# A graph-attention kernel on one core: later requests for block 2's rows, GpSimd's first sums beside the norms, a copy on ScalarE, and the last block's residual sums apart

## Chip, cores and metric

One core of one Trainium2 chip. The metric is device time in microseconds (us), one execution of the whole program. All arithmetic is fp32, and the matmuls decide the time: TensorE is busy for 2730.8 of the 2754.9 us of the kernel before.

## The reference, cut

x holds 128 graphs of 64 nodes with 768 features. It is normalised, passed through two attention layers over a 64 by 64 adjacency, and added to itself.

```python
h = jnp.maximum(_layernorm(x), 0.0)
for l in range(2):
    m_left  = jnp.einsum('bsh,oh->bso', h, W_left[l])
    m_right = jnp.einsum('bsh,oh->bso', h, W_right[l])
    u_left  = jnp.einsum('bih,bjh->bij', h, m_left) / temper
    u_right = jnp.einsum('bih,bjh->bij', h, m_right) / temper
    u = u_left * adj_tri + u_left * diag_mask + u_right * swapaxes(adj_tri, 1, 2)
    e = jnp.exp(u) * adj
    attention = e / (sum(e, axis=2, keepdims=True) + 1e-10)
    h_lin = jnp.einsum('bsh,oh->bso', h, W_lin[l]) + b_lin[l]
    h = relu(layer_norm(attention @ h_lin, ln_a[l], ln_b[l]))
return x + h
```

## The kernel before

The tokens are cut into 16 blocks of 512. For each layer a first pass projects a block with W_left and W_right and takes its scores; a second pass does W_lin, the context, the norm and, in layer 1, the residual sum. A projection is 15 block products instead of 18, on sums of weight blocks (`w_l`, `w_r`, `w_n`) and of token blocks (`ts`, from the transposed tokens `ht`); the products land in four PSUM banks X, Y, Z, V.

To place side work between matmuls, the program has numbered slots: two for each of the 15 products, slots 0 to 29 in the first half of a block and 30 to 59 in the second. `put(slot, f)` writes `f` there, so a larger number means a later place in the program. The residual sum of slot 22 runs behind VectorE's reads of bank X (2722.38 us behind 2721.72, kernel before).

The start (block 0): normalise, transpose on TensorE, copy out of PSUM, first sums.

```python
def scale(q0, q1):
    def deviation():
        nc.scalar.activation(sd[:, q0:q1], mv[:, q0:q1, 1], AF.Sqrt, bias=eps_in)
    def inverse():
        nc.vector.reciprocal(rs[:, q0:q1], sd[:, q0:q1])
        nc.vector.scalar_tensor_tensor(nb[:, q0:q1], mv[:, q0:q1, 0], -1.0, rs[:, q0:q1],
                                       op0=ALU.mult, op1=ALU.mult)
    return deviation, inverse
# ...
def turn(n, q):                       # transposes of one 128-row tile, then two copies
    # ...
        (nc.vector.tensor_copy if n < 2 else nc.scalar.copy)(
            to, p[:, :3 * P].rearrange("p (c a s) -> p c a s", c=3, a=2))
# ...
ws, vs = sums_w(0, "l", nc.gpsimd), sums_w(0, "l", nc.vector)
hold(KEEP["nb"][:, START[-2]:START[-2] + 1])     # GpSimd copies one column: it waits for the third nb
for f in ws[:2]:
    f()                                          # GpSimd's first two weight sums
```

The rows of the next block, in the first pass:

```python
def paced(to, f):
    nc.vector.memset(to, 0.0)         # the request f() must wait for this write
    f()

def prepare(u):
    todo = transpose_rows(l, u, sp)
    todo.append(lambda: load_h(1, l, u))
    if u + 1 < NB:
        todo.append(lambda: load_rows(l, u + 1, sp))    # 8 requests of 192 KB
    # ...
```

The last block of layer 1, and the end of the block before it, which runs beside it:

```python
def last_block(u):
    # ...
    put(20, lambda: load(0))
    for xs, slot in zip(XS[u, 1], (26, 45)):
        put(slot, lambda xs=xs: nc.gpsimd.tensor_add(xs, xs, rows["b"]))

def finish(u, r):
    # ...
    def scaled(k):
        nc.vector.scalar_tensor_tensor(zs[k], cx[k], rs[:, k:k + 1], rows["a"], op0=ALU.mult, op1=ALU.mult)
        nc.gpsimd.tensor_add(zs[k], zs[k], rows["b"])
    def done(k):
        xs = XS[u, r]
        nc.vector.scalar_tensor_tensor(xs[k], zs[k], 0.0, xs[k], op0=ALU.max, op1=ALU.add)  # residual sum
        # ... store xs[k]
        if k and u + r < NB - 1:
            residual(u + r, 1 - r)                # requests the rows of the next half: tile xr
    steps = [lambda f=f, k=k: f(k) for f in (scaled, done) for k in range(2)]
    return [inverse] + steps

# slots of inverse, scaled(0), scaled(1), done(0), done(1)
ends = ({0: ((u - 1, 0), (12, 13, 15, 22, 24)), 9: ((u - 1, 1), (28, 29, 30, 39, 41))},
        {2: ((u, 0), (44, 48, 51, 61, 62))})
```

Of the kernel before, what the change touches and what calls it, by code (L numbers as in the profile page):

```python
# [17 lines left out]
def kernel(  # L18
# [58 lines left out]
    def put(slot, *fs):  # L77
        plan.setdefault(slot, []).extend(fs)
# [164 lines left out]

    START = (0, 2, 1, 3)

    def load_rows(l, u, pool):

        XR[l, u] = []
        if (l, u) == (0, 0):

            rows = x.rearrange("(n k h) s f -> n k (h s) f", k=Q, h=PAIR)
            for g in range(2):
                t = pool.tile([P, 2, H], F32, name="x", bufs=2)
                XR[l, u].extend([t[:, 0, :], t[:, 1, :]])
            for q in START:
                nc.sync.dma_start(XR[l, u][q], rows[0, q])
            return
        for g in range(2):
            t = pool.tile([P, 2, H], F32, name="x", bufs=2)
            for a in range(4):  # L260
                i = 4 * g + a
                src = x[u * NBB + i] if l == 0 else ROWS[u][i]
                nc.sync.dma_start(t[a * 32:(a + 1) * 32], src.rearrange("(k j) h -> j k h", k=2))
            XR[l, u].extend([t[:, 0, :], t[:, 1, :]])

    def load_h(which, l, u):
        ht = HT[which, l, u] = big.tile([P, C, T], F32, name="ht")
# [11 lines left out]
    def transpose_rows(l, u, pool):  # L279

        key, xr, todo = (1, l, u), XR[l, u], []
        if l == 0:
            mv = stat.tile([P, Q, 2], F32, name="mv0", bufs=2)
            sd = stat.tile([P, Q], F32, name="sd0", bufs=2)
            rs = stat.tile([P, Q], F32, name="rs0", bufs=2)
            nb = stat.tile([P, Q], F32, name="nb0", bufs=2)
# [4 lines that stand above are left out]

                def inverse():
                    nc.vector.reciprocal(rs[:, q0:q1], sd[:, q0:q1])
                    nc.vector.scalar_tensor_tensor(nb[:, q0:q1], mv[:, q0:q1, 0], -1.0, rs[:, q0:q1],
                                                   op0=ALU.mult, op1=ALU.mult)

                return deviation, inverse

            def norm(q):
                nc.scalar.activation(xr[q], xr[q], AF.Relu, bias=nb[:, q:q + 1], scale=rs[:, q:q + 1])  # L300

            stats = [lambda q=q: mean_var(mv[:, q, :], [xr[q][:, :HH], xr[q][:, HH:]]) for q in range(Q)]
            norms = [lambda q=q: norm(q) for q in range(Q)]
            if u == 1:


                xb = pool.tile([P, H // 32, Q, 32], F32, name="xb", bufs=1)
                total, ss = (stat.tile([P, Q], F32, name=n, bufs=1) for n in ("total", "ss0"))

                def sums(q, to, **how):  # L310
                    nc.scalar.activation(xb[:, :, q, :], xr[q].rearrange("p (b j) -> p b j", j=32),  # L311
                                         accum_out=to[:, q:q + 1], **how)

                def inverse():
                    nc.scalar.activation(sd, ss, AF.Sqrt, bias=eps_in, scale=1.0 / H)
                    nc.vector.reciprocal(rs, sd)
                    nc.vector.tensor_mul(nb, total, rs)

                todo.extend([lambda q=q: sums(q, total, func=AF.Copy) for q in range(Q)])
                todo.append(lambda: nc.scalar.mul(total, total, -1.0 / H))  # L320
                todo.extend([lambda q=q: sums(q, ss, func=AF.Square, bias=total[:, q:q + 1]) for q in range(Q)])
                todo.extend([inverse, None] + norms)
            elif u:
                for f in stats + [lambda: [f() for f in scale(0, Q)]] + norms:
                    todo.extend([f, None])
            else:
                KEEP["nb"] = nb

                dev, inv = zip(*(scale(q, q + 1) for q in range(Q)))
                todo.extend([stats[START[0]], dev[START[0]]])  # L330
                for q, after in zip(START, START[1:] + (None,)):
                    if after is not None:
                        todo.append(stats[after])
                    todo.append(inv[q])
                    if after is not None:
                        todo.append(dev[after])
                    todo.append(norms[q])
        if (l, u) == (0, 0):
            ht = HT[key] = big.tile([P, C, T], F32, name="ht")

            def turn(n, q):

                if n < 2:
                    p = ps_aux.tile([P, 2, T], F32, name="aux")
                    banks = [p[:, 0], p[:, 1]]
                else:
                    banks = [ps_st.tile([P, 2 * TH], F32, name=m) for m in ("XY", "ZV")[n - 2]]
                for m, p in enumerate(banks):
                    for c in range(3):
                        nc.tensor.transpose(p[:, c * P:(c + 1) * P],  # L350
                                            xr[q][:, (3 * m + c) * P:(3 * m + c + 1) * P], KEEP["ident"])
                for m, p in enumerate(banks):
                    to = ht[:, 3 * m:3 * m + 3].rearrange("p c (a g s) -> p g c a s", a=4, g=2)
                    to = to[:, q // 2, :, q % 2 * 2:q % 2 * 2 + 2, :]
                    (nc.vector.tensor_copy if n < 2 else nc.scalar.copy)(
                        to, p[:, :3 * P].rearrange("p (c a s) -> p c a s", c=3, a=2))

            for n, q in enumerate(START):
                todo.append(lambda n=n, q=q: turn(n, q))
            todo.append(lambda: nc.sync.dma_start(KEPT[l][u], ht))  # L360
            return todo

        if (l, u) != (0, 1):
            xb = pool.tile([P, H // 32, Q, 32], F32, name="xb", bufs=1)

        def store():
            to = KEPT[l][u].rearrange("(b i) c t -> i c b t", b=4)
            for a in range(4):
                nc.sync.dma_start(to[:, :, :, a * P:(a + 1) * P],
                                  xb[a * 32:(a + 1) * 32].rearrange("i (c b) q j -> i c b (q j)", b=4))  # L370

        for q in range(Q):
            todo.append(lambda q=q: nc.vector.transpose(
                xb[:, :, q, :], xr[q].rearrange("p (b j) -> p b j", j=32)))
            todo.extend(none * ((l, u) != (0, 1)))
        todo.append(store)
        return todo

# [6 lines left out]
    def pass_one(l, aside):  # L385
        with tc.tile_pool(name=f"one{l}", bufs=2, reuse_waits="tile") as sp:
# [14 lines left out]

            def prepare(u):

                todo = transpose_rows(l, u, sp)
                todo.append(lambda: load_h(1, l, u))
                if u + 1 < NB:
                    todo.append(lambda: load_rows(l, u + 1, sp))
                todo.extend(softmax(u - 2) if u > 1 else [])
                todo.append(lambda: load_adj(u))
                todo.extend(none * ((9 if u > 1 else 15) if l else 0))  # L410
                return todo + affine(1, l, u)
# [86 lines left out]
            if l == 0:  # L498
# [18 lines left out]
                def hold(of):  # L517

                    t = stat.tile([P, 1], F32, name="hold", bufs=1)
                    nc.gpsimd.tensor_copy(t, of)  # L520
# [1 line left out]


                ws, vs = sums_w(0, "l", nc.gpsimd), sums_w(0, "l", nc.vector)
                hold(KEEP["nb"][:, START[-2]:START[-2] + 1])
                for f in ws[:2]:
                    f()
                t, w = deque(sums_t((1, 0, 0), nc.vector)), deque(vs[2:])
# [100 lines left out]
    def pass_two(l, aside):  # L629
        last = l == L - 1  # L630
        with tc.tile_pool(name=f"two{l}", bufs=2, reuse_waits="tile") as sp:
# [53 lines left out]
            def last_block(u):  # L685
# [12 lines left out]
                put(1, lambda: load(1))  # L698
                put(6, lambda: nc.gpsimd.tensor_scalar_mul(rows["-b"], rows["b"], -1.0))
                put(20, lambda: load(0))  # L700
                for xs, slot in zip(XS[u, 1], (26, 45)):
                    put(slot, lambda xs=xs: nc.gpsimd.tensor_add(xs, xs, rows["b"]))

            def finish_last(u, r):

# [155 lines left out]
            for u in range(NB):  # L861
# [21 lines left out]
                else:  # L883
                    if turn:
                        load_h(1, 1, 0)
                        put_all(28, affine(1, 1, 0), 3)
                        put_sums_t((1, 1, 0), 38, 2, 30)
                        ends = ({1: ((u - 1, 0), (13, 14, 16)), 11: ((u - 1, 1), (34, 35, 36))},
                                {4: ((u, 0), (50, 51, 52))})
                    else:  # L890
                        last_block(u)
                        ends = ({0: ((u - 1, 0), (12, 13, 15, 22, 24)), 9: ((u - 1, 1), (28, 29, 30, 39, 41))},
                                {2: ((u, 0), (44, 48, 51, 61, 62))})
                    linear(u, (0,), 0, ends[0], (1,))
                    linear(u, (1,), 30, ends[1], ())
# [52 lines left out]
```

## Time and profile before

| | before |
|---|---|
| median of the first 3 runs | 2756.12 us (2755.36 to 2756.13) |
| span of the profiled execution | 2754.9 us |
| TensorE busy | 2730.8 us, 99% |
| VectorE, ScalarE, GpSimd busy | 49%, 31%, 43% |

TensorE is full, so the time is its matmuls, which the change leaves alone, plus its pauses. Only what ends a pause of TensorE counts. The prediction below shows the three places with the largest pauses: the start, block 0's scores and the last block. Two more lines of the timeline also belong here. They are from the last block of the kernel before; the columns are start, duration, queue or engine, line, operation, tiles.

```profile
2726.89 2.52 SPq L732 DMA_DIRECT2D xr<-in_x_dram  x4
...
2732.72 2.16 DVE L816 SCALAR_TENSOR_TENSOR xr<-z,xr 128x768 f32<-128x768 f32 x1
```

The rows xr of the second half are requested from 2726.89 on, behind the second residual sum of the first half. In the transfer records the two requests for the first of its two tiles land by 2731.41; VectorE comes to them at 2732.72. So there were 1.3 us to spare (2732.72 - 2731.41).

### The profile page before, as it was taken

Reading aid. Unit: us, or ns where it says so; the run is one execution under the profiler, and the core shown is the slowest. Engines: PE = TensorE matmul, PEld = TensorE weight load, DVE = VectorE, ACT = ScalarE, POOL = GpSimd, SP = SyncE. Lnnn points to the kernel's source line nnn. Section 1 sums busy time; section 2 is a strip of 40 time slices with the busy share of each in tenths; the row PEclk is TensorE's granted clock in tenths of the full one; section 3 lists DMA queues with packets and bytes.
Section 4 is the critical chain, followed back from the end, with each engine's and each line's share of the span. In section 5 each row is a group of like instructions: output and inputs, shape, how many; then the busy total and the mean of one; then the engine's idle time right before and its main releaser. Section 6 shows DMA issues by size and latency. Waiting matters only on the chain.

```text
span 2754.9 us, 46440 instructions
## 1 busy us (share of the span) xinstructions
PE 2730.8 (99%) x18746; PEld 2343.7 (85%) x18746; DVE 1348.2 (49%) x2267; ACT 850.2 (31%) x1611; POOL 1195.0 (43%) x937
## 2 busy tenths in 40 slices
PE   9999999999999999999999999999999999999998
PEld 7888888888888888888788888888888888888886
DVE  6555445545454333333435444444444335676666
ACT  3222223222221154454621211121122214444443
POOL 3332352224223555555522344223222325887885
PEclk9999999999999999999999999999999999999999
DMA  6434433343332333343555433443344204555655
GB/s 203 121 75 97 121 82 81 87 120 93 76 76 77 102 104 121 119 146 123 152 129 150 99 75 76 109 119 78 76 98 120 59 26 146 167 165 164 178 161 144
DMA packets 234072, 310.82 MB, mean 113 GB/s; under 512 B 54146, under 2 KB 184450, under 8 KB 225666
## 3 DMA queue, kind: packets, MB, share of 16 engines
q1 hardware_dynamic: 233698, 307.45, 41.6%
q8 instruction: 149, 2.44, 0.4%
q14 instruction: 65, 0.53, 0.1%
q10 hardware_dynamic: 160, 0.39, 0.0%
HBM read 202.91 MB, written 104.86 MB: 112 GB/s over the span
## 4 chain that ended last, share of the span: by engine, by line
PE 96%; DVE 2%; ACT 1%; issue 1%; DMA 0%; SPq 0%; DVEq 0%; ACTq 0%
PE X L429 24%; PE V L429 16%; PE X L839 12%; PE Y L429 12%; PE Z L429 8%; PE V L839 8%; PE Y L839 6%; PE aux L456 5%; PE Z L839 4%; PE aux L654 2%; PE aux L677 1%; PE Y L677 0%; ACT xb L311 0%; DVE wm L470 0%; DMA x<-in_x_dram 0%
## 5 line engine op out<-in xcount | busy, mean ns | idle before, releaser
L155 POOL TENSOR_TENSOR ts<-ht 128x512 f32<-128x512 f32 x441 | 587.6, 1342 | 1223.0 <-DMA ht<-h 503.2
L203 ACT ACTIVATE m<-X 128x512 f32<-128x512 f32 (+1 forms) x256 | 151.7, 593 | 1089.9 <-PE X L429 571.2
L155 POOL TENSOR_TENSOR ts<-ht,ts 128x512 f32<-128x512 f32 x189 | 249.1, 1326 | 135.5 <-PE X L839 60.5
L155 DVE TENSOR_TENSOR m<-m,V 128x512 f32<-128x512 f32 (+1 forms) x256 | 173.4, 677 | 268.0 <-PE V L429 267.9
L155 DVE TENSOR_TENSOR m<-m,X 128x512 f32<-128x512 f32 (+1 forms) x256 | 162.9, 678 | 248.9 <-PE X L429 248.3
L839 PE MATMUL X<-w_n,ts 128*128 128x256 f32 x1024 | 244.2, 380 | 0.8 <-ACT hl L203 0.6
L429 PE MATMUL X<-ts,w_l 128*128 128x256 f32 x1024 | 242.7, 380 | 0.8 <-DVE ts L155 0.7
L429 PE MATMUL X<-ts,w_r 128*128 128x252 f32 (+1 forms) x1024 | 238.8, 376 | 0.1
L155 DVE TENSOR_TENSOR m<-m,Z 128x512 f32<-128x512 f32 (+1 forms) x128 | 87.5, 684 | 307.0 <-ACT m L203 248.7
L839 PEld LDWEIGHTS X<-w_n,ts 128*128 128x128 f32 x1024 | 191.5, 190 | 32.9 <-issue 3.1
L429 PEld LDWEIGHTS X<-ts,w_l 128*128 128x128 f32 x1024 | 192.0, 190 | 31.0 <-DVE m L155 2.7
L429 PEld LDWEIGHTS X<-ts,w_r 128*128 128x128 f32 x1024 | 192.0, 190 | 26.4 <-DVE m L155 0.5
L275 ACT ACTIVATE ht<-ht,b_col,a_col 128x512 f32<-128x512 f32 x192 | 143.5, 804 | 147.0 <-DMA ht<-h 147.0
L839 PE MATMUL Y<-w_n,ts 128*128 128x256 f32 x768 | 182.5, 379 | 0.0
L429 PE MATMUL Y<-ts,w_l 128*128 128x256 f32 x768 | 181.5, 379 | 0.2 <-DVE w_l L155 0.2
L429 PE MATMUL Y<-ts,w_r 128*128 128x252 f32 (+1 forms) x768 | 179.1, 376 | 0.0
L839 PEld LDWEIGHTS Y<-w_n,ts 128*128 128x128 f32 x768 | 145.8, 190 | 20.4 <-issue 0.6
L429 PEld LDWEIGHTS Y<-ts,w_l 128*128 128x128 f32 x768 | 145.8, 190 | 20.3 <-DVE w_l L155 0.6
L429 PEld LDWEIGHTS Y<-ts,w_r 128*128 128x128 f32 x768 | 145.9, 190 | 17.4
L155 DVE TENSOR_TENSOR hl<-hl,V 128x512 f32<-128x512 f32 (+1 forms) x136 | 89.1, 655 | 129.4 <-PE V L839 112.1
L805 POOL TENSOR_TENSOR z<-z,b 128x768 f32<-128x768 f32 x62 | 112.1, 1818 | 80.5 <-DVE z L802 80.5
L203 ACT ACTIVATE hl<-X 128x512 f32<-128x512 f32 (+1 forms) x135 | 78.0, 577 | 222.0 <-PE X L839 218.9
(165 smaller groups left out, 4741.1 us busy)
## 6 DMA issues: line engine op xcount, KB each, us to landing
ht<-h SPq DMA_DIRECT2D x63, 1536.0 KB, 7.1
h<-xb SPq DMA_DIRECT2D x124, 384.0 KB, 6.0
z<-z SPq DMA_DIRECT2D x128, 192.0 KB, 3.1
x<-z SPq DMA_DIRECT2D x128, 192.0 KB, 8.5
x<-in_x_dram SPq DMA_DIRECT2D x120, 192.0 KB, 8.3
xr<-in_x_dram SPq DMA_DIRECT2D x120, 192.0 KB, 3.7
out_dram<-xr SPq DMA_DIRECT2D x120, 192.0 KB, 2.7
adj<-in_adj_dram SPq DMA_DIRECT2D x64, 128.0 KB, 2.8
```

Of the source, the lines that this page charges most:

```text
L155: (eng.tensor_add if sign == "+" else eng.tensor_sub)(o, a, b)
L203: nc.scalar.activation(to(o), p, AF.Copy, scale=1.0 if sign == "+" else -1.0)
L275: nc.scalar.activation(ht, ht, AF.Relu, bias=cols[1][:, c:c + 1], scale=cols[0][:, c:c + 1])
L429: nc.tensor.matmul(p[:, g], w[ORDER[i][0]][:, c, g * P:(g + 1) * P], b()[t][:, c, :].rearrange(bs, s=S)[:, :, :ns], start=(new and g == c ...
L456: nc.tensor.matmul(p[h * S + e:h * S + e + 32, q, e:e + 95], ht[:, c, b * S + e:b * S + e + 32], mb[:, e:e + 95], start=(c == 0), stop=(c ...
L654: nc.tensor.matmul(cx[k][i, m, :HH], at[j, q, :], hl[j, q, m * HH:(m + 1) * HH], start=True, stop=True)
L677: nc.tensor.matmul(parts[r, k][n][i], at[j, q, :], hl[j, q, cut], start=True, stop=True)
L805: nc.gpsimd.tensor_add(zs[k], zs[k], rows["b"])
L839: nc.tensor.matmul(p[:, n], b[t][:, c, r * P:(r + 1) * P], w[s][:, c, :], start=(i in FIRST and i not in PRELOAD and n == c == 0), stop=(c ...
```

## The change

Its intent: to let GpSimd's first two weight sums run beside the norms; to have one of the first tile's two copies done by ScalarE; to request block 2's rows not before block 0's scores but behind them, so that they don't compete with TensorE's own instruction fetch (in the kernel before, a page of instructions started only at 73.24 us, as the data ended, and TensorE paused for 1.76 us); and to keep the residual sums of the last block but one, and GpSimd's bias adds, from running side by side (there a sum takes 2.02 us beside an add and 0.94 without; the prediction below shows what that costs).

```diff
--- before.py
+++ after.py
@@ -243,9 +243,9 @@
 
     START = (0, 2, 1, 3)
 
-    def load_rows(l, u, pool):
-
-        XR[l, u] = []
+    def load_rows(l, u, pool, now=True):
+
+        XR[l, u], ts = [], []
         if (l, u) == (0, 0):
 
             rows = x.rearrange("(n k h) s f -> n k (h s) f", k=Q, h=PAIR)
@@ -257,11 +257,16 @@
             return
         for g in range(2):
             t = pool.tile([P, 2, H], F32, name="x", bufs=2)
-            for a in range(4):
-                i = 4 * g + a
+            XR[l, u].extend([t[:, 0, :], t[:, 1, :]])
+            ts.append(t)
+
+        def load():
+            for i in range(NBB):
+                a = i % 4
                 src = x[u * NBB + i] if l == 0 else ROWS[u][i]
-                nc.sync.dma_start(t[a * 32:(a + 1) * 32], src.rearrange("(k j) h -> j k h", k=2))
-            XR[l, u].extend([t[:, 0, :], t[:, 1, :]])
+                nc.sync.dma_start(ts[i // 4][a * 32:(a + 1) * 32], src.rearrange("(k j) h -> j k h", k=2))
+
+        return load() if now else load
 
     def load_h(which, l, u):
         ht = HT[which, l, u] = big.tile([P, C, T], F32, name="ht")
@@ -291,6 +296,11 @@
 
                 def inverse():
                     nc.vector.reciprocal(rs[:, q0:q1], sd[:, q0:q1])
+                    if q1 - q0 == 1:
+
+                        nc.vector.tensor_scalar(nb[:, q0:q1], mv[:, q0:q1, 0], rs[:, q0:q1], -1.0,
+                                                op0=ALU.mult, op1=ALU.mult)
+                        return
                     nc.vector.scalar_tensor_tensor(nb[:, q0:q1], mv[:, q0:q1, 0], -1.0, rs[:, q0:q1],
                                                    op0=ALU.mult, op1=ALU.mult)
 
@@ -324,7 +334,6 @@
                 for f in stats + [lambda: [f() for f in scale(0, Q)]] + norms:
                     todo.extend([f, None])
             else:
-                KEEP["nb"] = nb
 
                 dev, inv = zip(*(scale(q, q + 1) for q in range(Q)))
                 todo.extend([stats[START[0]], dev[START[0]]])
@@ -334,6 +343,9 @@
                     todo.append(inv[q])
                     if after is not None:
                         todo.append(dev[after])
+                    if q == START[2]:
+
+                        todo.append(lambda: turn(0, START[0]))
                     todo.append(norms[q])
         if (l, u) == (0, 0):
             ht = HT[key] = big.tile([P, C, T], F32, name="ht")
@@ -352,10 +364,10 @@
                 for m, p in enumerate(banks):
                     to = ht[:, 3 * m:3 * m + 3].rearrange("p c (a g s) -> p g c a s", a=4, g=2)
                     to = to[:, q // 2, :, q % 2 * 2:q % 2 * 2 + 2, :]
-                    (nc.vector.tensor_copy if n < 2 else nc.scalar.copy)(
+                    (nc.vector.tensor_copy if n == 1 or n < m else nc.scalar.copy)(
                         to, p[:, :3 * P].rearrange("p (c a s) -> p c a s", c=3, a=2))
 
-            for n, q in enumerate(START):
+            for n, q in list(enumerate(START))[1:]:
                 todo.append(lambda n=n, q=q: turn(n, q))
             todo.append(lambda: nc.sync.dma_start(KEPT[l][u], ht))
             return todo
@@ -372,7 +384,7 @@
         for q in range(Q):
             todo.append(lambda q=q: nc.vector.transpose(
                 xb[:, :, q, :], xr[q].rearrange("p (b j) -> p b j", j=32)))
-            todo.extend(none * ((l, u) != (0, 1)))
+            todo.extend(none * ((l, u) not in ((0, 1), (0, 2))))
         todo.append(store)
         return todo
 
@@ -401,9 +413,14 @@
 
             def prepare(u):
 
-                todo = transpose_rows(l, u, sp)
+                todo = []
+                if (l, u) == (0, 2):
+
+                    load = load_rows(l, u, sp, False)
+                    todo = none + [lambda: paced(XR[l, u][0][:, :1], load)] + none * 9
+                todo.extend(transpose_rows(l, u, sp))
                 todo.append(lambda: load_h(1, l, u))
-                if u + 1 < NB:
+                if u + 1 < NB and (l, u) != (0, 1):
                     todo.append(lambda: load_rows(l, u + 1, sp))
                 todo.extend(softmax(u - 2) if u > 1 else [])
                 todo.append(lambda: load_adj(u))
@@ -522,7 +539,6 @@
 
 
                 ws, vs = sums_w(0, "l", nc.gpsimd), sums_w(0, "l", nc.vector)
-                hold(KEEP["nb"][:, START[-2]:START[-2] + 1])
                 for f in ws[:2]:
                     f()
                 t, w = deque(sums_t((1, 0, 0), nc.vector)), deque(vs[2:])
@@ -698,8 +714,15 @@
                 put(1, lambda: load(1))
                 put(6, lambda: nc.gpsimd.tensor_scalar_mul(rows["-b"], rows["b"], -1.0))
                 put(20, lambda: load(0))
-                for xs, slot in zip(XS[u, 1], (26, 45)):
-                    put(slot, lambda xs=xs: nc.gpsimd.tensor_add(xs, xs, rows["b"]))
+
+                def offset():
+
+                    t = stat.tile([P, 1], F32, name="hold", bufs=1)
+                    nc.gpsimd.tensor_copy(t, XS[u - 1, 1][1][:, :1])
+                    for xs in XS[u, 1]:
+                        nc.gpsimd.tensor_add(xs, xs, rows["b"])
+
+                put(42, offset)
 
             def finish_last(u, r):
 
@@ -889,7 +912,7 @@
                                 {4: ((u, 0), (50, 51, 52))})
                     else:
                         last_block(u)
-                        ends = ({0: ((u - 1, 0), (12, 13, 15, 22, 24)), 9: ((u - 1, 1), (28, 29, 30, 39, 41))},
+                        ends = ({0: ((u - 1, 0), (12, 13, 15, 19, 31)), 9: ((u - 1, 1), (28, 29, 30, 39, 41))},
                                 {2: ((u, 0), (44, 48, 51, 61, 62))})
                     linear(u, (0,), 0, ends[0], (1,))
                     linear(u, (1,), 30, ends[1], ())
```

In the last hunks the slots of `done(0)` and `done(1)` go from 22 and 24 to 19 and 31.

## The prediction

> **What bounds the kernel now.** I read the page first: the engines' busy shares, then the chain that ended last.
>
> ```profile
> PE 2730.8 (99%) x18746; PEld 2343.7 (85%) x18746; DVE 1348.2 (49%) x2267; ACT 850.2 (31%) x1611; POOL 1195.0 (43%) x937
> ...
> PE 96%; DVE 2%; ACT 1%; issue 1%; DMA 0%; SPq 0%; DVEq 0%; ACTq 0%
> ```
>
> TensorE is busy for 2730.8 of 2754.9 us and the chain is 96% TensorE. So 24.1 us is all that any change can win which leaves the matmuls alone, and this one does: on TensorE the orders of the two programs hold the same instructions in the same order. Where the 24.1 us lie I found by listing TensorE's records and every pause over 0.06 us between them: 1.4 us before its first instruction, 10.6 us after its last (it ends at 2744.3), and 21 pauses that sum to 11.8 us. Three places hold most of these, and they are the three that the change touches. The timeline shows them.
>
> The start:
>
> ```profile
> 10.15 0.19 POOL L520 COPY hold<-nb 128x1 f32<-128x1 f32 x1 [8.44 <-DVE nb L294]
> 10.30 2.50 POOL L155 TENSOR_TENSOR w_l<-w_l,w_l 128x512 f32<-128x512 f32 x2
> 10.34 1.24 DVE L294 SCALAR_TENSOR_TENSOR nb<-mv,rs 128x1 f32<-128x1 f32 x1
> 11.51 1.94 DVE L355 COPY ht<-aux 128x384 f32<-128x384 f32 x4
> 13.66 0.49 ACT L355 COPY ht<-V 128x384 f32<-128x384 f32 x1
> 14.32 1.97 PE L429 MATMUL X<-ts,w_l 128*128 128x256 f32 x8 [0.74 <-DVE ts L155]
> 23.37 1.97 PE L429 MATMUL X<-ht,w_l 128*128 128x256 f32 x8 [1.48 <-DVE w_l L155]
> ```
>
> Columns: start, duration, engine, line, operation, then in brackets the idle time and who ended it. The last nb, one element a lane, takes 1.24 us, because GpSimd's first sum starts 0.04 us ahead of it. Four copies of 0.485 follow, then VectorE's sums, and TensorE waits for VectorE at 14.32 and at 23.37.
>
> Block 0's scores, and block 1's beside them:
>
> ```profile
> 70.38 3.62 PE L456 MATMUL aux<-m,ht 128*32 128x95 f32 x163
> 75.76 0.85 PE L456 MATMUL aux<-m,ht 128*32 128x95 f32 x29 [1.76 <-issue]
> 128.13 4.13 PE L456 MATMUL aux<-m,ht 128*32 128x95 f32 x192
> ```
>
> The same 192 matmuls take 6.23 us in block 0 and 4.13 in block 1. After 163 of them TensorE stops for 1.76 us and waits for nothing that the profile shows ("issue"). The page's list of queues says what it may be:
>
> ```profile
> q8 instruction: 149, 2.44, 0.4%
> ```
>
> 149 packets of 16 KB: TensorE's instructions themselves. In the packet records one of these starts at 73.24, takes 1.21 us, and TensorE resumes 1.31 us after its end. In six later scores where a page falls alike, with quiet queues, the pause is 0.25 to 0.48 us, the page starts 1.0 to 1.75 us into the scores, and TensorE resumes 1.3 to 1.5 us after it has landed. So in block 0 the page started about 1.7 us late: the data queue was full until 73.25 with block 2's rows (issued 59.25 to 66.0 behind the load of ht) and adj.
>
> The last block:
>
> ```profile
> 2721.76 1.82 POOL L702 TENSOR_TENSOR ht<-ht,b 128x768 f32<-128x768 f32 x1 [0.61 <-DMA ht<-in_x_dram]
> 2722.38 2.02 DVE L816 SCALAR_TENSOR_TENSOR xr<-z,xr 128x768 f32<-128x768 f32 x1
> 2724.32 0.41 DVE L155 TENSOR_TENSOR hl<-hl,Y 128x256 f32<-128x256 f32 x1
> 2724.65 0.94 DVE L816 SCALAR_TENSOR_TENSOR xr<-z,xr 128x768 f32<-128x768 f32 x1
> 2725.52 0.41 DVE L155 TENSOR_TENSOR hl<-hl,V 128x256 f32<-128x256 f32 x1
> 2726.07 1.10 PE L839 MATMUL V<-w_n,ts 128*128 128x256 f32 x4 [1.88 <-DVE hl L155]
> ```
>
> The first residual sum takes 2.02 instead of 0.94 because GpSimd's add of the bias runs; behind it VectorE reads bank V late, and TensorE, which must write V again, waits 1.88 us.
>
> [...]
>
> **The change, part by part.**
>
> Start. GpSimd's hold goes, so its two sums run as soon as their weights are there (landed 8.76, 9.41 and 10.09): about 9.45 to 11.95 instead of 10.30 to 12.80. The nb becomes an operation with one SBUF tensor, so it need not wait: 0.16 instead of 1.24. One of VectorE's four copies goes to ScalarE. VectorE then: nb of the third tile ends at 10.0, one copy to 10.5, reciprocal and last nb to 10.8, two copies to 11.75; the first sum, held by GpSimd until 11.95, ends at 12.6 instead of 14.1. ScalarE: the copy enters at 10.04 and pushes the third norm to 10.41, but the fourth goes at 11.36 instead of 11.62 as its nb is not late; the last copy of the first tile then ends at 13.9 instead of 14.15. VectorE's second T sum needs that copy: it starts at 13.95 instead of 14.69. So of 1.5 us won on VectorE only 0.74 reach its chain of sums, and the pause of 23.37 shrinks by that. The transposes on TensorE end about 13.3 and its first matmul starts near 13.4 instead of 14.32, which is part of the same gain. **Start: -0.74 us.**
>
> Block 2's rows. They leave their place behind the load of ht (59.25) and are requested by a one-column memset on VectorE, which in the new order stands right behind the last read of bank V in block 0 (68.76 + 0.68). It waits for nothing on TensorE, so it runs near 69.45, 0.9 us before the scores begin, not after them. Requests then go out every 0.45 us, with first packets 1.0 us after the first (as for other requests of the trace): 70.5. The page is asked for near 71.3. By then two or three requests of 192 KB stand in the queues, less 0.75 us x 220 GB/s = 165 KB already moved: 220 to 410 KB, 1.0 to 1.9 us. If the page waits behind all of it, it starts at 72.3 to 73.2 and the pause is 0.9 to 1.75, a gain of 0 to 0.9.[...] I take **-0.9 us**.
> What it costs: the four transposes of block 2 move behind each other to the end of block 1's first half, 101.7 to 105.4 instead of ending at 97.9. The store (11.3 us to its last landing in block 1) and the load of ht (7.3) then end at 124.1, the first T sum on GpSimd (1.3) at 125.4, and TensorE needs it at 126.3. It fits by 0.9 us: **0**.
>
> Last block. The first residual sum moves from behind bank X's reads to ahead of them, the second into the second half; both GpSimd adds move behind the last sum of the block before, held by a copy of one column. VectorE: first sum from 2719.6, held by GpSimd's z until 2721.15, done near 2722.0; reads of X, Y, V follow TensorE, V at 2723.4 to 2723.8; TensorE ends Z at 2724.2 and goes on with V. The 1.88 us are gone. Everything later shifts; the two adds (2 x 1.82) run from about 2733.7 to 2737.4, just before GpSimd's z at 2737.4 to 2741.0, and the last sums start near 2741.0, against 2742.65 - 1.88 = 2740.8. **-1.75 us.**
>
> Sum: -0.74 - 0.9 - 1.75 = -3.4; 2756.1 - 3.4 = **2752.7 us**.
>
> **The rivals.** First, the rows still catch the page: the memset is off TensorE's order, and the page waits in line as before. For it: page 73.24 began just as the data ended. Then the scores stay near 6.2 us and the time is 2753.6. Second, a new wait at block 2: if store and load take over 0.9 us more than I think, TensorE waits at its first X matmul;[...] against: no competing load is left in that stretch. That gives 2753 to 2754.5. Third, the start's gain is eaten: VectorE's sums meet the weights' landings (up to 14.23) or GpSimd, and 23.37 stays; 2753.4. Fourth, all goes well, with the whole 1.76 and up to 1.3 at the start: 2751.3.
>
> **Range and chances.** The three gains have spans of 0.3 to 1.3, 0 to 1.7 and 1.0 to 1.9; runs of one kernel differ by 0.8 (2755.36 to 2756.13). I take 2750.8 to 2754.8. 2% is 55 us, more than twice all of TensorE's idle time, so faster by over 2% is out of reach, and nothing added is of that size: 0.005, 0.99, 0.005.
>
> **What would show it.** Right: last nb near 0.16 us, first T sum near 11.95, the pause of 23.37 down to about 0.7; block 0's scores at 5 to 5.8 us with the page starting 1 to 2 us into them; no pause over 0.2 us at the first matmuls of block 2; no pause before the V matmul of the last block's first half, with a residual sum ahead of it. Wrong: scores of 6.2 us, a wait for ts where block 2 begins, residual sums of 2 us or more which move the pause into the second half, or a time under 2750 or above 2755.

The sum stands as it was on record, -0.74 - 0.9 - 1.75 = -3.4 us, so 2752.7 us: none of its three terms is cut. The -0.9 for block 2's rows is the author's estimate. Two things that the prediction takes for granted need a figure. The nb of two tensors took 1.24 us beside GpSimd's sums in the kernel before (sums from 10.30 to 12.80) and 0.16 three times ahead of them; the changed form took 0.21 us beside them (9.49 to 11.99) and 0.21 three times ahead of them. And that the 149 packets are TensorE's instructions is the author's inference: TensorE has 2 x 18,746 records, 252 for each packet.

## The result

| | before | after |
|---|---|---|
| median (range), runs | 2755.74 (2754.63 to 2756.13), 4 | 2757.84 (2755.93 to 2758.76), 4 |
| span of the profiled execution | 2754.9 | 2754.1 |
| TensorE busy | 2730.8 | 2730.7 |

The ratio is 1.0007, with a 95% interval of 0.999 to 1.0025: the same within 2%, and not the gain of 3.4 us that was predicted. A ratio is here the mean time of one kernel's fast runs over that of the other's of the same rounds, so not quite the ratio of the medians quoted.

The profile's page of the changed kernel, busy shares and chain:

```profile
PE 2730.7 (99%) x18746; PEld 2343.7 (85%) x18746; DVE 1347.4 (49%) x2267; ACT 850.1 (31%) x1612; POOL 1194.1 (43%) x937
...
PE 96%; DVE 1%; DMA 1%; ACT 1%; issue 0%; SPq 0%; DVEq 0%; ACTq 0%
```

Nothing is to be seen at this level: shares of 2750 us don't show 2 us. What does show it is a comparison matmul by matmul. TensorE runs the same instructions in the same order in both kernels (18,746 matmuls in each trace), so each instruction has a start time in both traces. I call the difference the lead (negative: the changed kernel is earlier). It can change only where TensorE pauses or slows. Of the changed kernel's profile, the start, in the timeline:

```profile
9.49 2.50 POOL L155 TENSOR_TENSOR w_l<-w_l,w_l 128x512 f32<-128x512 f32 x2 [7.78 <-DMA w_l<-in_w_left_dram]
...
10.92 0.21 DVE L301 TENSOR_SCALAR nb<-mv,rs 128x1 f32<-128x1 f32 x1
...
12.10 0.69 DVE L155 TENSOR_TENSOR ts<-ht 128x512 f32<-128x512 f32 x1
...
12.96 1.94 PE L446 MATMUL X<-ts,w_l 128*128 128x256 f32 x8
...
13.74 0.69 DVE L155 TENSOR_TENSOR ts<-ht 128x512 f32<-128x512 f32 x1 [0.35 <-ACT ht L367]
...
22.42 1.97 PE L446 MATMUL X<-ht,w_l 128*128 128x256 f32 x8 [1.48 <-DVE w_l L155]
```

The last nb takes 0.21 us instead of 1.24, with GpSimd's sums beside it in both; GpSimd begins at 9.49 instead of 10.30, and the matmuls of 14.32 and 23.37 begin at 12.96 and 22.42. Lead at the end of the start: -0.95.

Block 0's scores, TensorE's timeline and SyncE's queue:

```profile
68.49 4.54 SPq L267 DMA_DIRECT2D x<-in_x_dram  x8
...
69.34 3.62 PE L473 MATMUL aux<-m,ht 128*32 128x95 f32 x163
74.19 0.85 PE L473 MATMUL aux<-m,ht 128*32 128x95 f32 x29 [1.22 <-issue]
```

The requests for block 2's rows go out 0.85 us before the scores begin, not behind them. The pause in the scores is 1.22 us instead of 1.76. Lead behind it: -1.57.

From there to the last block the lead grows by 1.9 us more, 1.6 of it in the other 31 scores, for a reason that is no part of the change. In both profiles the same 11 of these scores lose time, 0.1 to 0.8 us each; they are those in which TensorE's next page of instructions starts 1.0 to 1.75 us in. The other 20 take 4.13 us. What the 31 take over 4.13 us a piece sums to 3.9 to 6.3 us in the twelve profiles, and the changed kernel's first profile has the least, 3.9 (before: 5.4). That was luck. So a single pair of profiles carries an error of some 2 us, as large as any effect here, and spans must not be compared without taking it out.

The last block:

```profile
2716.07 2.42 DVE L839 SCALAR_TENSOR_TENSOR xr<-z,xr 128x768 f32<-128x768 f32 x1
...
2720.56 1.03 PE L862 MATMUL V<-w_n,ts 128*128 128x256 f32 x4
...
2723.82 1.94 DVE L839 SCALAR_TENSOR_TENSOR xr<-z,xr 128x768 f32<-128x768 f32 x1
...
2727.62 2.52 SPq L755 DMA_DIRECT2D xr<-in_x_dram  x4
...
2731.80 0.96 DVE L839 SCALAR_TENSOR_TENSOR xr<-z,xr 128x768 f32<-128x768 f32 x1 [4.58 <-DMA xr<-in_x_dram]
2732.67 0.41 DVE L155 TENSOR_TENSOR hl<-hl,V 128x256 f32<-128x256 f32 x1
...
2733.12 0.38 ACT L641 COPY V<-bias 128x256 f32<-128x256 f32 x1 [3.42 <-DVE hl L155]
...
2733.55 1.13 PE L862 MATMUL V<-w_n,ht 128*128 128x256 f32 x4 [2.54 <-ACT V L641]
...
2736.73 1.91 PE L862 MATMUL Y<-w_n,ts 128*128 128x256 f32 x4
```

Read from the top: the V matmul of the first half (2720.56) has no bracket any more; the pause of 1.88 is gone, and the lead grows from -3.47 to -5.59. Then, in the second half, VectorE is idle for 4.58 us, waiting for a transfer: the rows xr. Behind that residual sum stands VectorE's read of bank V; behind the read ScalarE's copy of the bias into V; behind the copy TensorE's next V matmul, which pauses for 2.54 us. The lead falls by 3.41. And the Y matmuls that follow take 1.91 us instead of 1.03. The granted clock shows why (the view of windows; the last columns are PEclk, DMA share and GB/s):

```profile
2733.00:2737.00 4.00, 2.86 (x9) 2.11 (x10) 3.21 (x8) 0.69 (x2) 2.67 (x3) 0.84 0.76 197
2737.00:2740.00 3.00, 3.00 (x10) 2.42 (x10) 2.21 (x5) 0.00 (x0) 3.00 (x3) 0.64 0.01 3
```

After the pause TensorE is granted half of its clock for 3.41 us, which costs another 1.62 us (8 matmuls start 0.43 us apart instead of 0.21). TensorE ends at 2743.55 against 2744.28: a lead of 0.73 us, of which, without the lucky scores, nothing would be left.

### The profile page after: what moved, and what is told of

Its sections match the earlier page's. It is cut to its first block, busy times and chain, and to the rows that moved or that the text cites. A ratio compares the mean times of both kernels' runs of the same rounds, so it can differ in the third digit from the quotient of the medians.

```text
span 2754.1 us, 46441 instructions
## 1 busy us (share of the span) xinstructions
PE 2730.7 (99%) x18746; PEld 2343.7 (85%) x18746; DVE 1347.4 (49%) x2267; ACT 850.1 (31%) x1612; POOL 1194.1 (43%) x937
## 4 chain that ended last, share of the span: by engine, by line
PE 96%; DVE 1%; DMA 1%; ACT 1%; issue 0%; SPq 0%; DVEq 0%; ACTq 0%
PE X L446 24%; PE V L446 16%; PE X L862 12%; PE Y L446 12%; PE Z L446 8%; PE V L862 8%; PE Y L862 6%; PE aux L473 5%; PE Z L862 4%; PE aux L670 2%; PE aux L693 1%; PE Y L693 0%; ACT xb L321 0%; DVE wm L487 0%; DMA w_l<-in_w_left_dram 0%
```

## The experiments

"Early" below is the kernel of the experiment early_rows, on which the later ones build.

**1. The change again.** No edit.

> The changed kernel unaltered, for a second profile and more times. Theory N (new wait): the last block's residual rows xr are requested behind the second residual sum, which the change moved from slot 24 to 31, so they land late; TensorE stands still for 2.5 us near the end and then runs 3.4 us at half clock, which gives back 5.0 us of the 5.6 won before. It expects the pause again, 2 to 4 us, and 2756 to 2759 us. Theory L (luck): the profiled execution lost time only by chance in its last block; then this profile has no pause over 1 us there, and the time is near 2753.

Measured: 2757.05 (2755.36 to 2758.14, 5 runs) against 2755.86 (2753.71 to 2757.76, 9 runs), ratio 1.0002 [0.999, 1.0015]. Its profile has the same course: lead -0.58 at the start, -1.60 behind the first scores, 2.12 us won in the last block's first half, then 3.15 lost around a pause of 2.36 us at the same V matmul. Here the clock stayed full (the first line is of the timeline, the second of the view of windows):

```profile
2735.18 1.13 PE L862 MATMUL V<-w_n,ht 128*128 128x256 f32 x4 [2.36 <-ACT V L641]
...
2735.00:2738.00 3.00, 2.25 (x9) 1.69 (x10) 2.97 (x7) 0.44 (x2) 2.05 (x3) 1.00 0.81 201
```

So the wait for xr belongs to the kernel; the halved clock is a second loss that comes with it or not. All nine runs of the change have a mean of 2757.09, all 23 of before 2755.63.

**2. The change without its part in the last block.**

```diff
-                put(42, offset)
+                for xs, slot in zip(XS[u, 1], (26, 45)):
+                    put(slot, lambda xs=xs: nc.gpsimd.tensor_add(xs, xs, rows["b"]))
...
-  ends = ({0: ((u - 1, 0), (12, 13, 15, 19, 31)), 9: ...
+  ends = ({0: ((u - 1, 0), (12, 13, 15, 22, 24)), 9: ...
```

> The change without its part in the last block (slots and bias adds as before). Theory N: the last block is as before, with its 1.9 us pause, and the start (-0.95 us in the profile after) and block 0's scores (-0.6) stay won: 1.6 us faster than before, 2753.5 to 2754.8. A rival, that the start or the moved rows cost time which the profile after hid: no faster than before.

Measured: 2754.84 (2754.18 to 2756.79, 5 runs), 0.9995 [0.9982, 1.0009]: 0.9 us under before in the means, not the 1.6 that I had expected, and not clear of noise. The old pause in the first half is back (2.00 us), and behind it, in the profiled run, the clock was halved for 3.41 us, at a cost of 1.68 us.

**3. The kernel before with the last block's part alone.** The two hunks of experiment 2, the other way, on the kernel before.

> The kernel before with the last block's part alone. Theory N: 2.1 us won in the first half of the last block, 5.0 lost in the second: 2.9 us slower than before, 2757.5 to 2759.5, with the 2.5 us pause and a stretch of half clock. If the loss needed the other parts (an earlier start, other transfers) it is faster than before by about 2 us.

Measured: 2757.64 (2755.84 to 2758.36, 5 runs), 1.0005 [0.9992, 1.0017]. In its profile 2.12 us are won in the first half and then 4.64 lost, at a pause of 2.75 us with the halved clock behind it. Experiments 2 and 3 together put the loss into the last block's part: the medians are 2757.1 and 2757.6 with it, 2754.8 and 2755.9 without it. Neither ratio is clear of noise alone; that the pause appears in all three profiles with this part, and in none of the three without it (before, before_again, no_last), is the stronger sign.

**4. The rows xr requested behind the first of the two residual sums.** Against the change:

```diff
-                        if k and u + r < NB - 1:
+                        if (k if (u, r) != (NB - 2, 0) else not k) and u + r < NB - 1:
                             residual(u + r, 1 - r)
```

> The changed kernel, with the residual rows of the last but one block's second half requested behind the first residual sum instead of the second, nothing else. Theory N: the wait of VectorE for these rows (4.6 us) and TensorE's pause of 2.5 us go, the clock stays whole to the end of the matmuls, and the time is 4 to 5 us below the changed kernel's: 2751 to 2753.5. If instead the pause comes of GpSimd's adds or of the order of VectorE's sums, it stays and the time is within 1 us of the changed kernel.

Measured: 2753.71 (2751.22 to 2753.77, 5 runs), 0.9989 [0.9977, 1.0002]; 3.7 us below the change in the same rounds (means 2753.00 and 2756.68). The timeline of the last block:

```profile
2719.89 2.52 SPq L755 DMA_DIRECT2D xr<-in_x_dram  x4
...
2727.32 1.11 DVE L839 SCALAR_TENSOR_TENSOR xr<-z,xr 128x768 f32<-128x768 f32 x1
...
2731.03 1.03 PE L862 MATMUL V<-w_n,ht 128*128 128x256 f32 x4
```

The request goes out 7.7 us earlier; VectorE's sum and TensorE's V matmul have no wait, the clock stays at 1.00, and the lead of -5.41 behind the first half lasts to the end (2738.88 against 2744.28). Nothing else was edited, so the late request was the cause of the loss, not the GpSimd adds that the change moved into the same stretch: they are still there.

**5. Block 2's rows requested truly behind the scores.** Against early: the write that the requests wait for is a copy out of the scores' own bank.

```diff
+                if (l, u) == (0, 0):
+                    KEEP["scored"] = p[:, 3, 40:41]
...
-  paced(XR[l, u][0][:, :1], load)
+  (nc.vector.tensor_copy(XR[l, u][0][:, :1], KEEP["scored"]), load())
```

> early_rows, with block 2's rows requested by a one-column copy out of the scores' own bank, which must wait for the last score, in place of the memset. Theory P (the page of instructions is held up by whatever data was requested before it): no rows are in the queues when the page is asked for, so the page starts 1.0 to 1.4 us into block 0's scores (1.7 to 2.0 in the four profiles with the memset), the pause there falls from 0.8 to 1.2 us to 0.2 to 0.5, and the time by 0.5 to 0.9 us. A rival, that the late page has nothing to do with the rows: start at 1.7 to 2.0 and a pause of 0.8 to 1.2 as before.

Measured: **2751.80** (2751.54 to 2752.04, 5 runs) against 2755.89 (10 runs), 0.9985 [0.9971, 0.9998]. It has the lowest median; early was not run in the same rounds (its mean was 1.2 us higher, with an error of 1.0). Block 0's scores, queue and TensorE:

```profile
69.30 4.54 PE L473 MATMUL aux<-m,ht 128*32 128x95 f32 x192
...
74.11 4.83 SPq L267 DMA_DIRECT2D x<-in_x_dram  x8
```

192 matmuls in one row: the largest pause left is 0.07 us, less than the 0.2 to 0.5 that I had expected. TensorE's instruction page starts 1.04 us into the scores. Block 2 still begins without a wait.

**6. Block 2's rows requested where before had them.** Against early, the edits of `prepare` and `transpose_rows` undone.

> early_rows, with block 2's rows requested where the kernel before did. Theory P: the page's start then depends on when the load of ht and the rows behind it end against the scores: 1.3 us (seen in last_only, pause 0.27) to 2.9 us (seen in before, pause 1.76). So the moved rows are worth between +0.6 and -0.9 us, nothing clear in the times: within 1 us of early_rows. If the change's placement were a plain gain of 0.9 us, as predicted, the pause is 1.6 us or more here again.

Measured: 2752.79 (2751.57 to 2753.79, 6 runs), 0.9987 [0.9975, 1.0]; not slower than early, which ran in other rounds. The scores:

```profile
69.30 3.62 PE L469 MATMUL aux<-m,ht 128*32 128x95 f32 x163
74.41 0.85 PE L469 MATMUL aux<-m,ht 128*32 128x95 f32 x29 [1.49 <-issue]
```

**7. The start as before.** Against early, the hunks on `inverse`, `turn` and `hold` undone.

> early_rows, with the start of the kernel before (hold on GpSimd, the two-tensor nb, four copies on VectorE). The start of the change was worth 0.95, 0.6 and 1.1 us of lead at 20 us in three profiles; so TensorE reaches the first X matmul on ht at 23.1 to 23.4 us here instead of 22.3 to 22.8, the last nb takes over 1 us, and the time is 0.6 to 1 us above early_rows. If the start is bound by the landing of the first rows instead, which differs by 0.4 us between executions, it is no later than there.

Measured: 2753.02 (2752.21 to 2754.12, 4 runs), 0.9989 [0.9976, 1.0003]. The times don't resolve the part. The timeline does, in part:

```profile
10.15 0.89 DVE L299 SCALAR_TENSOR_TENSOR nb<-mv,rs 128x1 f32<-128x1 f32 x1
...
22.82 1.53 PE L439 MATMUL X<-ht,w_l 128*128 128x256 f32 x6 [1.48 <-DVE w_l L155]
```

nb is blocked again (0.89 us), but the matmul at the end of the start begins at 22.82, a little earlier than I had expected: the start differs by some tenths between executions. All profiles together: the four with the old start have it at 22.82 to 23.55 (mean 23.21), the eight with the new one at 22.12 to 22.78 (mean 22.39). By these means the part is worth 0.8 us.

**8. The kernel before, one look.** No edit; a single run, so its state is unknown and only its course is used.

> The kernel before unaltered, for a second profile of it. Theory P: its pause in block 0's scores is not always 1.76 us: the page starts anywhere from 1.3 to 2.9 us into the scores. The last block's pause of 1.9 us, which comes of GpSimd's add, is there again. If 1.76 us is the rule, it is 1.6 to 1.9 here.

One time, 2758.25. Its trace shows that the kernel before itself falls into the halved clock:

```profile
2725.98 1.10 PE L839 MATMUL V<-w_n,ts 128*128 128x256 f32 x4 [2.22 <-DVE hl L155]
...
2728.34 1.91 PE L839 MATMUL Z<-w_n,ts 128*128 128x256 f32 x4
```

```profile
2726.00:2731.00 5.00, 5.00 (x16) 4.08 (x16) 2.97 (x7) 1.04 (x3) 2.39 (x2) 0.66 0.91 259
```

Its pause of the first half was 2.22 us instead of 1.88, and PEclk is 0.66 behind it, at a cost of 1.69 us. Block 0's scores had a pause of 1.49 us, so 1.76 is not the rule.

**9 and 10. Which of the two edits wins the first half?** Against early: only GpSimd's adds back at slots 26 and 45; only the sums back at slots 22 and 24.

```diff
 # adds_as_before
-                put(42, offset)
+                for xs, slot in zip(XS[u, 1], (26, 45)):
+                    put(slot, lambda xs=xs: nc.gpsimd.tensor_add(xs, xs, rows["b"]))
 # sums_as_before
-  ends = ({0: ((u - 1, 0), (12, 13, 15, 19, 31)), 9: ...
+  ends = ({0: ((u - 1, 0), (12, 13, 15, 22, 24)), 9: ...
```

> early_rows, with GpSimd's two bias adds back in their old places (slots 26 and 45, no hold). If the moved residual sums alone take away the 1.9 us pause of the first half (the first sum then runs before GpSimd's add, whose rows land later), TensorE has no pause over 0.5 us at the last V matmul of the first half, and the time is within 0.7 us of early_rows. If the adds are what matters (theory in the change's own words: residual sums apart), the pause is 1.5 to 2.2 us there again.

> early_rows, with the residual sums back in slots 22 and 24, the moved adds kept. With GpSimd's add gone from there, the first sum takes 0.94 instead of 2.02 us. If the adds alone are enough, the pause of 1.9 us falls under 0.9 us; by my count of VectorE's row (two sums of 0.94 and the reads of Y, V and Z behind X's reads) 0.8 us remain, and the time is 0.5 to 1 us above early_rows.

Measured: 2753.00 (2752.71 to 2754.05, 5 runs), 0.9994 [0.998, 1.0007], and 2754.13 (2752.44 to 2755.88, 5 runs), 0.9996 [0.9984, 1.0009], both against 2755.06 (9 runs). They were run on another chip. On the other chip early did not run, so their courses decide and not their times. With the adds back nothing is lost: the lead in the first half goes by -2.12 as in early. With the sums back it goes by -1.06 only, and half of the pause remains:

```profile
2720.94 0.95 DVE L839 SCALAR_TENSOR_TENSOR xr<-z,xr 128x768 f32<-128x768 f32 x1
...
2723.57 1.10 PE L862 MATMUL V<-w_n,ts 128*128 128x256 f32 x4 [0.82 <-DVE hl L155]
```

The sum takes 0.95 us there, without a GpSimd add beside it, against 2.02 before. So what makes the pause is the place of two sums ahead of bank V's read (0.8 us) and the block by GpSimd (1.1 us); moving the sums removes both, moving the adds only the second.

## Why the prediction was wrong

The start. Predicted -0.74; measured -0.95 in the first profile and -0.83 on average. The chain was right: sums at 11.95 and 13.95 were predicted, 12.10 and 13.74 measured, nb 0.21 us. One step was wrong. The pause in front of the matmul of 23.37 did not shrink to 0.7; it is 1.48 in both. I had let VectorE's chain come earlier and left TensorE where it was, but TensorE's first matmuls also begin 1.36 us earlier, so both ends of that pause moved together, and 0.43 us was given back at a Y matmul whose pause grew from 0.16 to 0.59.

Block 2's rows. Predicted -0.9; the term was mis-sized. That the requests would go out 0.9 us before the scores was right (0.85 measured), and in the first pair of profiles the scores fell from 6.23 to 5.69 us, which lies within what the prediction allowed. But 6.23 was the longest of four. Four profiles with the requests in the old place have scores of 6.23, 5.95, 5.95 and 4.74 us (mean 5.72), seven with the change's memset 5.29 to 5.69 (mean 5.49): the part is worth 0.2 us, far less than the four differ among themselves. Truly behind the scores it is 4.54 (one profile). TensorE's page of instructions starts 1.35 to 2.86 us into the scores in the old place, 1.68 to 2.03 with the memset, 1.04 with empty queues, and in all twelve profiles the pause is that start less 0.7 to 1.1 us. So the first rival was mostly right, the rows still catch the page, though in another way: new rows instead of old ones. With the old place the page comes when the data end: it starts 5.2 to 5.4 us behind the last request for adj in all four profiles. That is why it came early, at 1.35, in last_only: there the row of requests from ht on began 12.8 us ahead of the scores, in the other three 11.6. One count of the prediction was wrong: it names six later scores with a pause of 0.25 to 0.48; in its trace seven of those in which a page starts 1.0 to 1.75 us in have one, of 0.25 to 0.49, and four have none over 0.06.

Block 2's beginning. Predicted 0; there is no pause over 0.06 us there. The second rival fell.

The last block, the step that failed: "The 1.88 us are gone. Everything later shifts". The first sentence held, and to the tenth: the first residual sum was put at 2719.6 to 2722.0 in the time of the profile before, and it ran at 2719.54 to 2721.96 (2716.07 to 2718.49 plus the lead of 3.47). The gain was 2.12, predicted 1.75. The second sentence did not hold, because one thing did not shift along. I followed the sums and GpSimd's adds through the slots, not the request that hangs on the second sum. In before it went out at 2726.89, with 1.3 us to spare at its use. In after it goes out at 2727.62, while TensorE's program is 5.59 us ahead: in the program's own time it is 0.73 + 5.59 = 6.3 us later. In the last_only profile the same sum is 2.93 + 3.41 = 6.3, so it is no accident of one execution. About 1 us of it is an estimate for the second sum itself, which took 1.94 us instead of 0.94: it runs beside GpSimd's add on z (2723.12 to 2727.43). 1.3 - 6.3 leaves 5.0 us short; VectorE waited 4.58. All of this could have been worked out from the timeline of before: it holds the request, the landing and the use.

The price: 3.15 and 3.41 us for the wait in the change's two profiles, and in one of them 1.62 us more for the halved clock; last_only loses 4.64 for both. Set against 2.12 won, the part loses 1.0 to 2.9 us instead of winning 1.75. With the terms re-sized: -0.8 - 0.2 - 2.1 + 3.2 to 5.0 = +0.1 to +1.9 us. Measured, over all fast runs, 2757.09 - 2755.63 = +1.5, with an error of some 0.9 us (twice the standard error from the runs' spread). In the same rounds alone it is 2757.09 - 2755.87 (13 runs) = +1.2, with an error of 1.0. So the sum is confirmed in sign and rough size, not to the tenth.

The prediction had named, among what would show it wrong, a pause that moves into the second half, but by residual sums of 2 us or more, and a time above 2755. The pause did move there. The sums that wait are 0.96 us long; what came late was their data. (A sum of 1.94 us does stand there, but ahead of the request, not of the pause.)

The halved clock was in no rival. In the six profiles with a pause of 1.8 to 2.8 us in the last block, before (1.88) and after_again (2.36) kept the full clock; no_last (2.00), before_again (2.22), after (2.54) and last_only (2.75) did not. The length alone does not sort them. The clock records lie on a grid of 3.413 us whose phase differs between executions (the half clock is recorded from 2735.73 to 2739.14 in after, and behind the last matmul from 2745.97 there and from 2748.30 in before); TensorE's idle time within one interval of it was 1.66 and 1.55 us in the two that kept the clock, and 1.82 to 2.75 in the four that lost it. The ends of the programs, where TensorE stops within some interval, agree in all twelve profiles: behind an interval with 1.73 us idle (no_last) or less the clock stays full, behind one with 1.80 (before_again) or more it is halved, and no other interval after the first clock record breaks this. So the border lay between 1.73 and 1.80 us of idle time in one interval: the author's estimate from these twelve traces, which no run was made to test. The halved clock may be one reason why runs of the kernel before spread over 4 us (2753.71 to 2757.76), since its pause of about 2 us (1.88 and 2.22 in its two profiles) lies near that border; runs without a profile can't show it.

The combination that the change was after does exist: with xr requested early and block 2's rows truly behind the scores, 2751.80 us, 4.3 us under before in the same rounds (means 2751.77 and 2756.05; still within the 2% that count as the same), and with the narrowest spread of all, 0.5 us. That no pause near 2 us is left in its last block agrees with that; the trace alone does not prove that the spread comes from it.

## What to carry to other kernels

When a piece of work moves to a later place in an engine's program, list what hangs on it, requests first: a transfer issued behind the moved instruction moves too, and it need not shift along with the engines that got faster: here xr was requested 0.73 us later while TensorE was 5.59 us ahead. Compare request, landing and use in the program's own time, before and after. And where a request must stand behind some matmuls, make it wait for their result: behind a memset that depended on none of the scores the requests went out 0.85 us before them (68.49 against 69.34), behind a copy out of the scores' bank after them (74.11, the scores ending at 73.84).
